# Fused GroupNorm and multi-head attention on one core: the last two batches' softmax denominators in another order, and two edits at the start

## The chip, the cores and the metric

The kernel runs on one core of a Trainium2 chip, all in float32. The metric is the device time of one execution in microseconds (us), lower is better. The kernel before takes 1836.15 us (median of three runs, 1836.12 to 1836.40). The profile shown is of one execution of it, which took 1836.99 us; the span that the profiler recorded inside it is 1835.3 us, and the granted TensorE clock was 0.997 of full speed.

The engines are named as in the profile: PE is TensorE (matrix products, with PEld its weight loads), DVE is VectorE, ACT is ScalarE, POOL is GpSimd, and SP is the sync engine, which here only issues DMA transfers. Each engine works through its own instructions in order and waits on semaphores for the others. A `q` behind an engine's name marks its queue of DMA issues and the like.

## The reference

The input x has 32 batches of 256 channels by 32x32 positions. Each batch is normalized in groups of 8 channels, projected to queries, keys and values of 8 heads of 32 channels, put through causal attention that leaves out the diagonal too, and added to x:

```python
q = einsum('oc,bcs->bos', q_w, gn(x)) + q_b        # gn: GroupNorm of 32 groups
k, v = split(einsum('oc,bcs->bos', kv_w, gn(x)) + kv_b)
scores = einsum('bhqd,bhkd->bhqk', q, k) / sqrt(32)
scores = where(mask == 0, -10000.0, scores)        # mask: tril(ones(1024, 1024), -1)
attn = where(mask == 0, 0.0, softmax(scores))
out = x + einsum('bhqk,bhkd->bhqd', attn, v)
```

## The kernel before

**Tiling.** A batch has two groups of four heads (`g`) and two halves of 512 query positions (`hf`), so its output has four quarters, numbered `n = 2 * g + hf`; each is 128 channels by 512 positions. Scores are computed transposed, keys on partitions. A batch is cut into twelve *visits*. At a visit `scores` (L290) issues the products of one full and one half piece of scores, ACT takes their exponentials (L319, L321), POOL masks what lies on the diagonal (`mask`, L283), and the products with the values (`values`, L332) of the visit before are issued. There is one running loop over `i` from 0 to 384 (32 x 12 visits and one more for the last values).

**Numerator and denominator.** TensorE adds the values' products of a quarter in one PSUM tile, and ACT copies it to `num` (L351). The softmax denominators are sums of exponentials over the keys. The keys' sum over pieces is made by DVE (`total += e`, L348), which leaves 128 partial sums for each query. There are then two ways to the end:

- *Folded*, for batches 0 to 29: `fold` (L358) adds the upper half of the partitions to the lower with an accumulating DMA from POOL, twice (512 KB, then 256 KB). `stack` (L364) brings the 32 rows that are left into one tile `folded` by a DMA from SP. `sum_folded` (L370) transposes and reduces on DVE, once for each of four heads. `check_sums` (L431) tests the range, `invert` (L437) takes the reciprocal, turns it (L446), writes it to DRAM with four small DMAs (L448) and reads it back with four broadcasts (L453, 256 KB each), which spread each head's row over its 32 partitions into `rb`.
- *Late*, for batches 30 and 31: `sums` (L401) adds up the keys with products on TensorE (`sum_keys`, L383) into the one spare PSUM bank, ACT copies it to `den` (L416), and SP writes 4 rows of it to DRAM (L419). `gather` (L424) reads them back as rows of 64, and `check_sums` and `invert` follow without the turning (one small write, L443, then the broadcasts of L453).

`finish` (L462) multiplies numerator and inverse (L466), adds the values' bias and x (L467), copies one column (L469), all on DVE, and stores the quarter (L470). In the last batch, quarters 0 and 1 go through `finish_aside` (L472) instead: POOL multiplies and adds (L477, L478), ACT adds the bias (L479), SP stores (L482). Quarters 2 and 3 of the last batch have their sums on all partitions already and are checked and inverted on the spot (`check_here` L484, `invert_here` L491, reciprocal L493). `end_last` (L495) does this for quarter 3 in two halves of 256 columns and puts one number, `outside`, together, which tells whether any sum left the range (the kernel then runs a slow general form; here it never does).

**What sets the order.** PE, ACT, DVE and POOL keep the order in which the program issues their instructions. That order is written out with `when(i, f, at)` and `when(i, f, after)`: `f` is called at visit `i`, behind its scores, or after the visit's values. The numbers stand in the tables PROJECT, PREPARE, SUMS and FINISH (L545 to L549), and the main part fills them for each batch. SP's order is set by a scheduler, mostly by when an issue's inputs are ready; the issues of SP then go out in that order too, each waiting for its own semaphores. Buffers: `folded` has one, `den` two, `rb` and the half exponentials `eh` four each.

**Start.** `load(0)` brings in x_0, `load_weights` (L122) the weights from SP and the three bias vectors from ACT's queue (L126 to L128). x_0 goes through statistics (L166), mean and variance, `norm_apply`, then the first projections, in the order of `projections` (L245), and the first scores.

Of the kernel before, what the change touches and what calls it, by code (L numbers as in the profile page):

```python
# [17 lines left out]
P = 128  # L18
# [13 lines left out]
def tile_norm_attention_residual(  # L32
# [64 lines left out]
    def unshifted():  # L97
# [24 lines left out]
        def load_weights():  # L122
            for n, w in enumerate((q_w, kv_w[0:C], kv_w[C : 2 * C])):
                live["wn", n] = epool.tile([P, 4, HALFBANK], F32, tag="eh", bufs=4, name=f"wn_{n}")[:, :NG, :C]
                nc.sync.dma_start(out=live["wn", n], in_=w.rearrange("(o p) c -> p o c", p=P))
            nc.scalar.dma_start(out=qk_bias[:, 0, :], in_=q_b.rearrange("(g p) -> p g", p=P))  # L126
            nc.scalar.dma_start(out=qk_bias[:, 1, :], in_=kv_b[0:C].rearrange("(g p) -> p g", p=P))
            nc.scalar.dma_start(out=v_bias_col, in_=kv_b[C : 2 * C].rearrange("(g p) -> p g", p=P))  # L128

        def turn_weights(n):  # L130
            wn = live["wn", n]
# [109 lines left out]
        def projections(b):  # L241

            qk = [[lambda g=g, hf=hf, n=n: project_qk(b, g, n, hf) for n in range(2)] for g in range(NG) for hf in range(NH)]
            v = [lambda n=n: project_v(b, n) for n in range(NB // 2)]
            return qk[0] + qk[1][:1] + v[:2] + qk[1][1:] + qk[2] + v[2:] + qk[3]  # L245

# [152 lines left out]
        def sums(b, g, hf):  # L401

            n = NH * g + hf
            den = small.tile([P, HALF], F32, tag="den", name=f"den_{b}_{n}")
            if (b, n) == (B - 1, 3):
                pd = live["pd", b]
            else:
                pd = misc(f"pd_{b}_{n}")
                sum_keys(pd, live.pop(("sum", b, g, hf)), slice(0, HALF), slice(0, HALF))
            if b == B - 1 and n >= 2:  # L410

                most = small.tile([P, 1], F32, tag="most", name=f"most_{n}")
                nc.scalar.activation(den, pd, AF.Identity, accum_out=most)
                live["most", n], live["den", n] = most, pd if n == 3 else den
                return
            nc.scalar.copy(den, pd)  # L416
            if n == 0:
                live["sums", b] = dram.tile([4, 4, HALF], F32, tag="sums", name=f"sums_{b}")
            nc.sync.dma_start(out=live["sums", b][n], in_=den[::HD, :])  # L419
# [17 lines left out]
        def invert(b, ns):  # L437
            part = slice(ns.start * HD, ns.stop * HD)
            inv = small.tile([P, ROW], F32, tag="inv", name=f"inv_{b}_{ns.start}")
            nc.vector.reciprocal(inv[part], live["rows", b][part])  # L440
            live["inv", b] = dram.tile([4, 4, HALF], F32, tag="inv", name=f"inverses_{b}_{ns.start}")
            if b >= B - 2:
                nc.sync.dma_start(out=spread_rows(live["inv", b])[part], in_=inv[part])  # L443
            else:
                turned = small.tile([P, ROW], F32, tag="inv_turned", name=f"inv_turned_{b}")
                nc.vector.transpose(turned, inv)  # L446
                for n in ns:
                    nc.sync.dma_start(  # L448
                        out=live["inv", b][n].rearrange("(a j) (m c) -> (j m) a c", a=2, c=HD),
                        in_=turned[n * HD : (n + 1) * HD].rearrange("p (a c) -> p a c", a=2),  # L450
                    )
            for n in ns:
                nc.sync.dma_start(  # L453
                    out=inverses(b, n),
                    in_=live["inv", b][n].unsqueeze(1).broadcast_to([4, HD, HALF]),
                )

        def inverses(b, n):
            live["rb", b, n] = work.tile([P, HALF], F32, tag="rb", bufs=4, name=f"rb_{b}_{n}")
            return live["rb", b, n]  # L460

        def finish(b, n, within=slice(0, HALF)):  # L462
# [6 lines left out]
                nc.vector.tensor_copy(rb[:, 0:1], xt[:, g, 0:1])  # L469
            nc.sync.dma_start(out=x_out[b, :, g, cols], in_=rb)  # L470

        def finish_aside(b, n, within=slice(0, HALF)):  # L472

            g, hf = divmod(n, NH)
            cols = slice(hf * HALF + within.start, hf * HALF + within.stop)
            num, rb, xt = live["num", b, n], live["rb", b, n][:, within], live["x", b]
            nc.gpsimd.tensor_tensor(rb, num[:, within], rb, ALU.mult)  # L477
            nc.gpsimd.tensor_tensor(rb, rb, xt[:, g, cols], ALU.add)  # L478
            nc.scalar.activation(rb, rb, AF.Identity, bias=v_bias_col[:, g : g + 1])  # L479
            if cols.start == 0:  # L480
                nc.scalar.copy(rb[:, 0:1], xt[:, g, 0:1])
            nc.sync.dma_start(out=x_out[b, :, g, cols], in_=rb)  # L482

        def check_here(n, ok):  # L484
# [4 lines left out]
            nc.vector.scalar_tensor_tensor(ok, live["most", n], SUM_MAX, least, ALU.is_le, ALU.mult)  # L489

        def invert_here(b, n, within):  # L491
            rb = live["rb", b, n] if within.start else inverses(b, n)
            nc.vector.reciprocal(rb[:, within], live["den", n][:, within])  # L493

        def end_last(b):  # L495

# [1 line left out]
            worst = const.tile([P, 1], F32, name="worst")  # L498
            ok = const.tile([P, 1], F32, name="ok")
            nc.vector.tensor_reduce(worst, in_range, AX.X, ALU.min)  # L500
            check_here(3, ok)
            both = [slice(c * HALFBANK, (c + 1) * HALFBANK) for c in range(2)]
            invert_here(b, 3, both[0])
            pc = ps_o.tile([P, HALF], F32, tag="acc", name="pc")
            nc.tensor.matmul(pc[0:1, 0:1], lhsT=worst, rhs=ok, start=True, stop=True)
            outside = const.tile([1, 1], I32, name="outside")
            nc.vector.tensor_scalar(outside, pc[0:1, 0:1], -1.0, float(P), ALU.mult, ALU.add)
            finish_aside(b, 3, both[0])
            invert_here(b, 3, both[1])
            finish(b, 3, both[1])  # L510
            return outside

# [30 lines left out]


        PROJECT = (-5, -4, -3, -2, -1, 0, 1, 2, 3, 4, 5, 6)  # L545
        PREPARE = (-16, -15, -9, -9, -8, -8, -7, -6, -5, -4)
        SUMS = (3, 7, 9, 13)

        FINISH = ((N + 13, N + 13, N + 14, N + 15), (N + 7, N + 7, N + 8, N + 9))  # L549
        every = range(4)  # L550

        with tc.manual_schedule(engines={ENG.PE, ENG.Activation, ENG.DVE, ENG.Pool}):
# [7 lines left out]
            keep_busy(11)  # L560
            for g in range(NG):
                norm_channels(0, g)
            nc.vector.tensor_scalar_mul(qk_bias[:, 0, :], qk_bias[:, 0, :], SCALE)
            norm_mean(0)
            keep_busy(3)
            norm_deviation(0)
# [5 lines left out]
            for hf in range(NH):  # L572
                for g in range(NG):
                    norm_apply(0, hf, g)
            units = projections(0)
            for n, f in zip((None, None, 0, 0, 0, 0) + PROJECT[6:], units):
                if n is None:
                    f()
                else:
                    when(n, f)  # L580
            if B > 1:
                prepare(1, (None, None, 0, 1, 2, 2, 3, 4, 5, 6))
            for b in range(B):
                first, last, late = b * N, b == B - 1, b >= B - 2
                if b >= 1:
                    for n, f in zip(PROJECT if not last else PROJECT[:-1] + (8,), projections(b)):
                        when(first + n, f)
# [2 lines left out]
                    prepare(b, [first + n for n in PREPARE])  # L590
                for n in every:
                    v = first + (N if last and n == 3 else SUMS[n])
                    if late:
                        when(v, lambda b=b, n=n: sums(b, *divmod(n, NH)), after)
                    else:
                        when(v, lambda b=b, n=n: fold(b, n, 2 * HD), after)
                        when(v + 2, lambda b=b, n=n: fold(b, n, HD), after)
                        when(v + 4, lambda b=b, n=n: stack(b, n))
                if not last:
                    if late:  # L600
                        when(first + N + 2, lambda b=b: gather(b, every))
                    else:
                        when(first + N + 6, lambda b=b: sum_folded(b, every[:2]), after)
                        when(first + N + 7, lambda b=b: sum_folded(b, every[2:]), after)
                    v = first + N + (4 if late else 8)
                    when(v, lambda b=b: check_sums(b, every))
                    when(v, lambda b=b: invert(b, every))
                    for n in every:
                        when(first + FINISH[late][n], lambda b=b, n=n: finish(b, n), after)
                else:  # L610
                    when(first + N - 4, lambda b=b: gather(b, every[:2]))
                    when(first + N - 3, lambda b=b: check_sums(b, every[:2]))
                    when(first + N - 3, lambda b=b: invert(b, every[:2]))
                    when(first + N, lambda b=b: check_here(2, in_range[:, ROW : ROW + 1]))
                    when(first + N, lambda b=b: invert_here(b, 2, slice(0, HALF)))
                    when(first + N, lambda b=b: finish(b, 2))
                    for n in every[:2]:
                        when(first + N, lambda b=b, n=n: finish_aside(b, n), after)
            for i in range(B * N + 1):
                if i < B * N:  # L620
                    scores(i // N, *visits[i % N])
# [1 line left out]
                    f()  # L623
                for n, pc in enumerate(products[(i - 1) % N] if i else ()):

                    summed = i < B * N - 2 or (i == B * N - 2 and n == 0)
                    values((i - 1) // N, pc, summed)
                    if i == B * N:
                        sum_piece(B - 1, pc, stop=n == 1)
                        if n == 0:  # L630
                            sum_total(B - 1)
                if i == B * N - 1:
                    for n, pc in enumerate(products[N - 2] + products[N - 3][1:]):
                        sum_piece(B - 1, pc, start=n == 0)
                for f in after.pop(i, ()):
                    f()
# [159 lines left out]
```

## Time and profile before

| | |
|---|---|
| time, median of 3 | 1836.15 us |
| span of the profiled execution | 1835.3 us |
| one regular batch (visit to the same visit of the next) | 55.98 us |
| start of the first scores | 18.28 us |
| end of the last product | 1822.4 us |
| end of DVE's last operation | 1830.86 us |
| last store issued | 1830.89 us |

The page counts the busy time of each engine and follows back the chain of work that ended last. A row of a timeline gives the start in us, the length in us, the engine, the line of the program, the operation, what it writes and reads, and in brackets the idle time before it and what ended that. With "x4" several neighbours are merged in one row. Because the tail is short against the whole, the averages of the page say little on it; the timelines of the first 20 and the last 120 us are what bears on this change.

### The profile page before, as it was taken

Reading aid. Unit: us, or ns where it says so; the run is one execution under the profiler, and the core shown is the slowest. Engines: PE = TensorE matmul, PEld = TensorE weight load, DVE = VectorE, ACT = ScalarE, POOL = GpSimd, SP = SyncE. Lnnn points to the kernel's source line nnn. Section 1 sums busy time; section 2 is a strip of 40 time slices with the busy share of each in tenths; the row PEclk is TensorE's granted clock in tenths of the full one; section 3 lists DMA queues with packets and bytes.
Section 4 is the critical chain, followed back from the end, with each engine's and each line's share of the span. In section 5 each row is a group of like instructions: output and inputs, shape, how many; then the busy total and the mean of one; then the engine's idle time right before and its main releaser. Section 6 shows DMA issues by size and latency. Waiting matters only on the chain.

```text
span 1835.3 us, 53874 instructions
## 1 busy us (share of the span) xinstructions
PE 1815.7 (99%) x23200; PEld 925.6 (50%) x23200; DVE 1650.8 (90%) x1747; ACT 1481.1 (81%) x1871; POOL 797.1 (43%) x772
## 2 busy tenths in 40 slices
PE   8999999999999999999999999999999999999997
PEld 5454555554554555555545545555545455455443
DVE  3789999999999999999999999999999999999878
ACT  5888878888788888788887888887888877888775
POOL 1444534434434445344354344454453543444414
PEclk9999999999999999999999999999999999999999
DMA  3447676666666676766667666767667666667412
GB/s 121 69 84 137 136 154 113 127 135 139 143 127 120 136 139 136 152 113 128 135 139 145 128 121 134 139 135 152 114 125 139 137 143 133 119 134 138 88 51 84
DMA packets 77518, 231.46 MB, mean 126 GB/s; under 512 B 20288, under 2 KB 21312, under 8 KB 61912
## 3 DMA queue, kind: packets, MB, share of 16 engines
q0 software_dynamic: 15360, 94.39, 37.2%
q1 hardware_dynamic: 61096, 133.54, 24.3%
q8 instruction: 184, 3.01, 0.7%
q14 instruction: 62, 0.51, 0.1%
q10 hardware_dynamic: 816, 0.00, 0.0%
HBM read 67.42 MB, written 34.64 MB: 56 GB/s over the span
## 4 chain that ended last, share of the span: by engine, by line
PE 96%; DVE 3%; ACT 1%; issue 0%; DMA 0%; SPq 0%; DVEq 0%; ACTq 0%
PE sT L269 31%; PE acc L343 26%; PE pp L156 25%; PE ppv L156 13%; DVE e L348 1%; DVE rb L493 0%; DVE rb L466 0%; ACT e L321 0%; DMA x<-in_x_dram 0%; DVE rb L467 0%; PE pv L156 0%; ACT eh L319 0%; PE pd L383 0%; PE wt L135 0%; PE pm L156 0%
## 5 line engine op out<-in xcount | busy, mean ns | idle before, releaser
L321 ACT ACTIVATE e<-sT 128x1024 f32<-128x1024 f32 x768 | 745.9, 1025 | 274.6 <-PE sT L269 202.5
L348 DVE TENSOR_TENSOR e<-e,e 128x1536 f32<-128x1536 f32 x381 | 638.8, 1677 | 20.3 <-POOL e L283 2.7
L348 DVE TENSOR_TENSOR e<-e,eh 128x1024 f32<-128x1024 f32 x381 | 523.9, 1389 | 133.6 <-PE acc L343 113.6
L283 POOL TENSOR_SCALAR_AFFINE_SELECT e<-e 128x512 f32<-128x512 f32 (+1 forms) x256 | 379.4, 1482 | 591.6 <-ACT e L321 571.6
L269 PE MATMUL sT<-q,k 32*128 32x256 f32 (+3 forms) x7168 | 607.2, 458 | 0.8 <-ACT k L223 0.8
L269 PEld LDWEIGHTS sT<-q,k 32*128 32x128 f32 x7168 | 443.0, 184 | 158.0 <-ACT eh L319 65.6
L156 PE MATMUL pp<-xn,wT 128*32 128x512 f32 x4096 | 492.3, 598 | 0.2 <-ACT den L416 0.2
L343 PE MATMUL acc<-e,v 128*32 128x512 f32 (+2 forms) x4096 | 400.7, 486 | 0.0
L319 ACT ACTIVATE eh<-sT 128x1024 f32<-128x1024 f32 x384 | 397.6, 1036 | 0.0
L362 POOL DMA_DIRECT2D e<-e x240 | 196.6, 824 | 377.7 <-DMA e<-e 301.4
L156 PE MATMUL ppv<-wT,xn 128*32 128x256 f32 x4096 | 247.3, 382 | 0.0
L343 PEld LDWEIGHTS acc<-e,v 128*32 128x32 f32 x4096 | 132.5, 110 | 223.4 <-issue 192.1
L343 PE MATMUL acc<-eh,v 128*32 128x256 f32 x3072 | 224.4, 379 | 0.0
L156 PEld LDWEIGHTS pp<-xn,wT 128*32 128x32 f32 x4096 | 107.0, 109 | 220.0 <-issue 204.6
L343 PEld LDWEIGHTS acc<-eh,v 128*32 128x32 f32 x3072 | 98.4, 110 | 165.0 <-issue 152.9
L156 PEld LDWEIGHTS ppv<-wT,xn 128*32 128x32 f32 x4096 | 120.2, 109 | 103.1 <-issue 28.8
L283 POOL TENSOR_SCALAR_AFFINE_SELECT eh<-eh 128x512 f32<-128x512 f32 x128 | 165.8, 1295 | 0.2
L209 ACT ACTIVATE xn<-x,shift,rstd 128x512 f32<-128x512 f32 x124 | 103.3, 833 | 0.0
L467 DVE SCALAR_TENSOR_TENSOR rb<-rb,v_bias_col,x 128x512 f32<-128x512 f32 x126 | 95.8, 761 | 4.5
L223 ACT ACTIVATE q<-pp,qk_bias 128x512 f32<-128x512 f32 x128 | 91.2, 712 | 2.5 <-DVE st L166 2.5
L223 ACT ACTIVATE k<-pp,qk_bias 128x512 f32<-128x512 f32 x128 | 89.8, 702 | 2.2 <-PE pm L156 1.1
L466 DVE TENSOR_TENSOR rb<-num,rb 128x512 f32<-128x512 f32 x126 | 88.1, 700 | 0.1
(69 smaller groups left out, 671.5 us busy)
## 6 DMA issues: line engine op xcount, KB each, us to landing
e<-e POOLq DMA_DIRECT2D x120, 512.0 KB, 6.3
x<-in_x_dram SPq DMA_DIRECT2D x64, 512.0 KB
out_dram<-rb SPq DMA_DIRECT2D x127, 256.0 KB
rb<-inverses SPq DMA_DIRECT2D x126, 256.0 KB
e<-e POOLq DMA_DIRECT2D x120, 256.0 KB, 4.8
folded<-e SPq DMA_DIRECT2D x120, 256.0 KB
inverses<-inv_turned SPq DMA_DIRECT2D x120, 8.0 KB
wn<-in_L_conv_kv_w_dram SPq DMA_DIRECT2D x2, 256.0 KB
```

Of the source, the lines that this page charges most:

```text
L156: nc.tensor.matmul(out[part], lhsT=lhsT[:, part], rhs=rhs, start=start, stop=stop, skip_group_check=True)
L209: nc.scalar.activation(xn, xt, AF.Identity, bias=live["shift", b][:, g : g + 1], scale=rstd)
L223: nc.scalar.activation(live[key][:, cols], pp, AF.Identity, bias=qk_bias[:, n, g : g + 1], scale=(SCALE, 1.0)[n],)
L269: return nc.tensor.matmul(pair[:, cols], lhsT=live["k", b, g][rows, kb * P : (kb + 1) * P], rhs=live["q", b, g][rows, hf * HALF + of.start ...
L283: nc.gpsimd.affine_select(out=diagonal, in_=diagonal, pattern=[[0, 4], [0, n], [1, P]], compare_op=ALU.is_gt, fill=0.0, base=0, channel_mu ...
L319: exp = nc.scalar.activation(eh.rearrange("p (n bank) q -> p bank n q", n=2), short, AF.Exp)
L321: nc.scalar.activation(e[:, 2 * a : 2 * a + 2, :], pairs[a], AF.Exp)
L343: nc.tensor.matmul(acc[HD * j : HD * (j + 1), of], lhsT=live["v", b][:, kb, h * HD : (h + 1) * HD], rhs=e[:, j, cols], start=first, stop=l ...
L348: nc.vector.tensor_add(total[:, :, of], total[:, :, of], e[:, :, cols])
L362: nc.gpsimd.dma_start(out=total[:rows], in_=total[rows : 2 * rows], accum_op=ALU.add)
L466: nc.vector.tensor_mul(rb, num[:, within], rb)
L467: nc.vector.scalar_tensor_tensor(rb, rb, v_bias_col[:, g : g + 1], xt[:, g, cols], ALU.add, ALU.add)
```

## The change

1. The three bias loads go from ACT's queue to SP's, behind the weights. The scaling of q's bias by DVE moves from ahead of the mean to behind the first half's `norm_apply`.
2. In every batch the first V unit of the projections is issued one place earlier; for batch 0 it thereby stands ahead of the first scores. The last step of PREPARE moves one visit later.
3. Batch 30 takes the folded way like batches 0 to 29. Its sums by TensorE fall away; its folds, stacks, `sum_folded`, turning and four broadcasts come in. Its four `finish` move from visits 379, 379, 380, 381 to 381, 381, 382, 382.
4. The last batch's quarters 0 and 1 are gathered, checked and inverted one at a time (0 at visits 379 and 380, 1 at 380 and 381), into one tile `rb_last` that takes `folded`'s place. `finish_aside` is split: the part on POOL for quarter 0 goes to the end of visit 382, ahead of the masks of visit 383.
5. Check and reciprocal of quarter 2 move from visit 384 to 382. From visit 382 on the exponentials' sums of the last batch are made by TensorE alone (before, one piece of that visit was still added on DVE).
6. In `end_last` the reciprocal of the first half comes ahead of the check, and the second half's ahead of `outside`.

```diff
-            nc.scalar.dma_start(out=qk_bias[:, 0, :], in_=q_b.rearrange("(g p) -> p g", p=P))
...
+            nc.sync.dma_start(out=qk_bias[:, 0, :], in_=q_b.rearrange("(g p) -> p g", p=P))
...
-            return qk[0] + qk[1][:1] + v[:2] + qk[1][1:] + qk[2] + v[2:] + qk[3]
+            return qk[0] + v[:1] + qk[1][:1] + v[1:2] + qk[1][1:] + qk[2] + v[2:] + qk[3]
...
-            if b >= B - 2:
+            if b == B - 1:
                 nc.sync.dma_start(out=spread_rows(live["inv", b])[part], in_=inv[part])
...
+            if b < B - 1:
+                live["rb", b, n] = work.tile([P, HALF], F32, tag="rb", bufs=4, name=f"rb_{b}_{n}")
+            else:
+                if n == 0:
+                    live["rb_last"] = work.tile([P, 4, HALF], F32, tag="folded", bufs=1, name="rb_last")
+                live["rb", b, n] = live["rb_last"][:, n, :]
...
+            inverses(b, 3)
+            invert_here(b, 3, both[0])
+            quotient_aside(b, 3, both[0])
             check_here(3, ok)
-            both = [slice(c * HALFBANK, (c + 1) * HALFBANK) for c in range(2)]
-            invert_here(b, 3, both[0])
+            invert_here(b, 3, both[1])
...
-            finish_aside(b, 3, both[0])
-            invert_here(b, 3, both[1])
+            out_aside(b, 3, both[0])
             finish(b, 3, both[1])
...
-        PREPARE = (-16, -15, -9, -9, -8, -8, -7, -6, -5, -4)
+        PREPARE = (-16, -15, -9, -9, -8, -8, -7, -6, -5, -3)
...
-        FINISH = ((N + 13, N + 13, N + 14, N + 15), (N + 7, N + 7, N + 8, N + 9))
+        FINISH = ((N + 13, N + 13, N + 14, N + 15), (N + 9, N + 9, N + 10, N + 10))
...
-            nc.vector.tensor_scalar_mul(qk_bias[:, 0, :], qk_bias[:, 0, :], SCALE)
             norm_mean(0)
...
-            for n, f in zip((None, None, 0, 0, 0, 0) + PROJECT[6:], units):
+            for n, f in zip((None, None, None, 0, 0, 0) + PROJECT[6:], units):
...
-                    if late:
+                    if last:
                         when(v, lambda b=b, n=n: sums(b, *divmod(n, NH)), after)
...
+                    when(first + N + 6, lambda b=b: sum_folded(b, every[:2]), after)
+                    when(first + N + 7, lambda b=b: sum_folded(b, every[2:]), after)
+                    when(first + N + 8, lambda b=b: check_sums(b, every))
+                    when(first + N + 8, lambda b=b: invert(b, every))
...
-                    when(first + N - 4, lambda b=b: gather(b, every[:2]))
-                    when(first + N - 3, lambda b=b: check_sums(b, every[:2]))
-                    when(first + N - 3, lambda b=b: invert(b, every[:2]))
-                    when(first + N, lambda b=b: check_here(2, in_range[:, ROW : ROW + 1]))
-                    when(first + N, lambda b=b: invert_here(b, 2, slice(0, HALF)))
+                    for n in every[:2]:
+                        when(first + N - 5 + n, lambda b=b, n=n: gather(b, every[n : n + 1]))
+                        when(first + N - 4 + n, lambda b=b, n=n: check_sums(b, every[n : n + 1]))
+                        when(first + N - 4 + n, lambda b=b, n=n: invert(b, every[n : n + 1]))
+                        when(first + N - 2 + 2 * n, lambda b=b, n=n: quotient_aside(b, n), after)
+                        when(first + N - 1 + n, lambda b=b, n=n: out_aside(b, n), after)
+                    when(first + N - 2, lambda b=b: check_here(2, in_range[:, ROW : ROW + 1]))
+                    when(first + N - 2, lambda b=b: inverses(b, 2))
+                    when(first + N - 2, lambda b=b: invert_here(b, 2, slice(0, HALF)))
                     when(first + N, lambda b=b: finish(b, 2))
-                    for n in every[:2]:
-                        when(first + N, lambda b=b, n=n: finish_aside(b, n), after)
...
-                    summed = i < B * N - 2 or (i == B * N - 2 and n == 0)
-                    values((i - 1) // N, pc, summed)
+                    values((i - 1) // N, pc, i < B * N - 2)
...
-                    for n, pc in enumerate(products[N - 2] + products[N - 3][1:]):
+                    for n, pc in enumerate(products[N - 2] + products[N - 3]):
```

## The prediction

> **What bounds the kernel now.** I read the page first.
>
> ```profile
> PE 1815.7 (99%) x23200; PEld 925.6 (50%) x23200; DVE 1650.8 (90%) x1747; ACT 1481.1 (81%) x1871; POOL 797.1 (43%) x772
> PE 96%; DVE 3%; ACT 1%; issue 0%; DMA 0%; SPq 0%; DVEq 0%; ACTq 0%
> ```
>
> TensorE is busy 99% of the span and is 96% of the chain: over the body only less TensorE work, or less waiting of it, saves time. But DVE ends the chain. The chain of waits from 1815 us on is DVE without a break:
>
> ```profile
> 1814.77 2.28 DVE e L348
> ...
> 1818.74 3.27 DVE rb L493
> ...
> 1822.04 1.72 DVE rb L466
> ...
> 1828.21 1.69 DVE rb L493
> ...
> 1830.38 0.48 DVE rb L467
> ```
>
> TensorE's last product ends at 1822.4. DVE's timeline has no idle beyond 0.5 us from 1783.23 to 1830.86; then the last store is issued, and the span ends at 1835.3. So what the tail costs is read on DVE from 1783 on, not on TensorE.
>
> What the early denominators of batch 30 cost now stands in TensorE's timeline:
>
> ```profile
> 1721.45 1.04 PE L383 MATMUL pd<-e,pick 128*32 128x512 f32 x8
> 1723.20 0.24 PE L156 MATMUL pm<-mv,avg 128*32 128x2 f32 x8 [0.70 <-ACT den L416]
> ```
>
> Eight more matmuls, then a wait for ACT to empty the bank. Last, the DMA queues. SP's timeline around batch 28's inverses, and the stretches after it (us; busy PE, PEld, DVE, ACT, POOL; clock, DMA share, GB/s):
>
> ```profile
> 1747.06 2.59 SPq L448 DMA_DIRECT2D inverses<-inv_turned  x4
> 1750.40 2.58 SPq L453 DMA_DIRECT2D rb<-inverses  x4
> 1755.44 0.51 SPq L419 DMA_DIRECT2D sums<-den  x1
> ```
>
> ```profile
> 1754.00:1756.00 2.00, 2.00 (x24) 1.07 (x16) 1.90 (x2) 0.70 (x2) 0.00 (x0) 1.00 0.26 99
> 1760.00:1762.00 2.00, 2.00 (x44) 1.40 (x40) 1.90 (x2) 1.17 (x2) 0.00 (x0) 1.00 0.26 98
> 1764.00:1766.00 2.00, 2.00 (x28) 1.25 (x28) 1.98 (x1) 0.95 (x2) 0.62 (x1) 1.00 0.00 0
> ```
>
> Four broadcasts of 256 KB go at 98 GB/s with a DMA share of 0.26, that is on 4 of 16 engines: 1.05 MB / 98 GB/s = 10.7 us. The landing signals in the trace agree: first issue 1750.40, landings 1755.21, 1757.89, 1760.56, 1763.22 (4.8 us, then 2.67 each). The 8 KB write of L419 issued behind them at 1755.44 landed at 1763.40, where such a write otherwise takes 1.2 to 1.7 us.
>
> **What the skill says.** "DMA: Bandwidth & Descriptors", section "Why a DMA increments its semaphore by 16 and not by 1": a DMA from SP runs on k engines, the largest number up to 16 that divides both slowest dimensions, and on the lowest-numbered k. A broadcast whose source begins with 4 heads gets k = 4; the trace agrees (0.26). The same page, "Queues, rings and completion order": each engine takes its descriptors in ring order. So a 16-engine transfer issued behind four broadcasts has a quarter of its pieces behind them. The trace agrees: the store issued at 1814.88 landed at 1820.85, just after the broadcast ahead of it (1820.33); stores otherwise take some 1.7 us. "SBUF — State Buffer", "Who interferes with whom": a DVE operation with two SBUF inputs and a GpSimd operation that reads SBUF exclude each other. The trace agrees: L466 takes 0.68 us alone, 1.71 beside L477/L478.
>
> **The change, part by part.** Working in the clock of before's trace.
>
> *Start.* TensorE's idle of 0.81 us ahead of the first scores (they wait for `k L223`) is filled by the V unit that comes from behind them: −0.8. The bias loads are 816 packets of 4 bytes on ACT's queue between 2.96 and 7.86 us, among x_0's. x_0's second half landed at 6.98; from 2 to 5 us the core moved 209, 238 and 148 GB/s, later 330 to 400. At 350 that shortfall of 455 KB is 1.3 us. So the gain is 0 to 1.3; I take 1.0, as the chain goes from x_0 through statistics and `norm_apply` to the first product. L563 (0.12 us) leaves that chain, or lies beside it. Start: −1.8.
>
> *Batch 30 folded.* Visits of batch 30 that hold the extra sums, against the same visit of a regular batch: 363 6.89 / 5.13, 367 5.95 / 4.66, 368 4.49 / 4.22, 369 6.82 / 5.08, 373 5.90 / 4.65. The differences, 1.76 + 1.29 + 0.27 + 1.74 + 1.25 = 6.31 us, leave TensorE. Added: eight accumulating DMAs on POOL (0.82 us of issue each, POOL 43% busy; every earlier batch does it in the regular 55.98 us per batch) and four stacks on SP: hidden by TensorE. Added on DVE: four pairs of transpose and reduce, 0.70 + 0.69 each, 5.55; turning 0.24; and the rest of `invert(30)` moves from 1786.89 (0.87 us) to visit 380. They fall in the stretch where DVE never rests, so they count in full.
>
> *Last batch in two parts.* DVE: one more check and reciprocal, 0.9, since 32 rows cost about what 64 do (0.21 + 0.22 + 0.54, overlapped); the key sums of visit 381's products leave it: −2.28. TensorE gets 0.86 more of L383, hidden by DVE's tail. Net on DVE with the former part: 5.55 + 0.24 + 0.9 − 2.28 = +4.4.
>
> *The new wait, which decides.* In the built SP order the four small writes, the inverses of (31, 0), the four broadcasts of batch 30, a fifth broadcast (31, 0), and only then the gather of `rows` (31, 1) follow each other. `check_sums` of (31, 1) at visit 381 waits for that gather on DVE; queued behind it are the key sums of 381, all four `finish(30)`, the last halves and the end. Step by step:
> - `sum_folded(30)` ends: 1802.00 (where L466 stood) − 0.87 + 5.55 = 1806.7.
> - check, invert, turn: 1.15 (1745.80 to 1746.95 in batch 28): 1807.9.
> - From the end of turning to the first broadcast 2.0 to 3.5 us in the trace; I take 2.9: 1810.8.
> - Four landings by +12.8, the fifth 2.67 later, the gather with it: about 1826.5. (Alone it lands 2.2 us after issue, 1806.38 to 1808.6.)
> - DVE has check (31, 0) and the sums of 380 (0.9 + 2.4) until 1811.2, then nothing: 15.3 us idle.
> - After it: check and invert 1.0; sums of 381 2.3; four finishes 6.0 (0.68 + 0.75 each, 0.15 twice); check of 2 0.9; reciprocal 3.34; finish (31, 2) 1.6; worst 0.2; reciprocal 1.75; check of 3 0.85; reciprocal 1.75; outside 0.1; last finish 0.9: 20.7. The two POOL quotients (2.55 each) now lie beside these: from 0 to 5.1 more; I take 3.6, as half of DVE's operations there have two SBUF inputs. DVE ends at 1850.8.
> - The end follows 4.4 later (1830.86 to 1835.3): 1855.2. Less 6.31 and 1.8: 1847.1.
>
> Before's span is 1835.3 and the runs have 1836.15, 0.85 more: **1848**. That is 11.8 us slower. Its own range: gather 2 us sooner to 1 later, contention 0 to 5.1, start 0.8 to 2.1: 1843.5 to 1852.5.
>
> **Rivals.** A (same, 1838): the gather isn't held, because its pieces run beside the broadcasts. It would land at 1814.5 + 2.2 = 1816.7; DVE idles 5.5, and the end comes at 1816.7 + 20.7 + 3.6 + 4.4 − 8.1 + 0.85 = 1838.1. For: 12 of its 16 engines are free. Against: the two held transfers above.
>
> B (same to slower, 1837 to 1842): POOL decides. The quotient of (31, 0) stands ahead of visit 383's masks and waits for the fifth broadcast (1826.3); + 2.55 + 1.8 for the masks gives 1830.7; then about 4 us of values and sums, 6 of the last half's DVE work, 4.4: 1845 to 1850 − 8.1 + 0.85. It decides only when DVE comes through sooner than this.
>
> C (faster, 1832.5): nothing idles on DVE. A without its 5.5 us, or 1835.3 + 4.4 − 8.1 + 0.85: DVE's extra work eats most of what TensorE gives. For: DVE's tail is dense now, so it needs broadcasts and gather to land while DVE has other work. Against: `finish(30)`, which could fill the gap, is queued behind the waiting check. It decides if the gather is issued 5 us earlier than I read.
>
> **How the numbers follow.** Forecast 0.78, A 0.08, B's milder loss 0.08, C 0.06. Two runs differ by 0.02%, but I count 0.2% (3.7 us) as what tells from no change. Slower: 0.78 plus 0.06 of B = 0.84; same: A and 0.02 of B, 0.10; faster: 0.06. Range: forecast's 1843.5 to 1852.5 holds 0.9 of 0.78; down to 1838 it takes in B and half of A: 1838 to 1853 holds about 0.82.
>
> **What would show it.** Right: a gap of some 15 us on DVE ahead of the second L434 of batch 31, ended by a DMA on `rows`; a DMA share near 0.26 for 13 us before; scores of visit 372 starting about 8 us earlier (6.3 + 1.8); first scores with no wait for `k`. Wrong: a gap under 6 us there (A), masks of visit 383 as the last releaser of the end (B), or a chain that ends on TensorE. If visit 372 isn't 7 to 9 us earlier, the folding or start term is wrong.

## The result and the profile after

The changed kernel takes 1847.98 us (median of six runs, 1846.84 to 1848.69) against 1836.30 for the kernel before (1836.12 to 1836.75): a ratio of 1.0063, 95% interval 1.0050 to 1.0076. That is 11.7 us slower, where 11.8 was forecast. The profiled execution took 1848.65 us, with a span of 1846.9.

The totals and the chain of the page, to hold against those of before:

```profile
PE 1813.4 (98%) x23176; PEld 925.4 (50%) x23176; DVE 1658.0 (90%) x1758; ACT 1481.6 (80%) x1867; POOL 799.8 (43%) x780
PE 97%; DVE 2%; DMA 1%; SPq 0%; issue 0%; ACT 0%; DVEq 0%
```

TensorE does 2.3 us less and the span is 11.6 us longer. DMA, 0% of the chain before, is now 1% of it. The chain's own view of the last 60 us says which:

```profile
1805.88 11.54 DMA rows<-sums
...
1817.44 1.31 DVE in_range L434
```

`rows<-sums` is the gather of quarter 1 of the last batch: 8 KB, 11.54 us. DVE's timeline shows the hole that it leaves:

```profile
1799.77 2.41 DVE L348 TENSOR_TENSOR e<-e,e 128x1536 f32<-128x1536 f32 x2
1817.44 1.30 DVE L434 SCALAR_TENSOR_TENSOR in_range<-rows,in_range 32x64 f32<-32x64 f32 x1 [15.26 <-DMA rows<-sums]
...
1841.81 0.48 DVE L472 SCALAR_TENSOR_TENSOR rb_last<-rb_last,v_bias_col,x 128x256 f32<-128x256 f32 x1
```

And SP's timeline shows what was issued ahead of the gather; the stretches below it (same columns as in the prediction) show how long that took:

```profile
1799.07 1.77 SPq L448 DMA_DIRECT2D inverses<-inv_turned  x4
1800.88 0.42 SPq L443 DMA_DIRECT2D inverses<-inv  x1
1801.40 2.59 SPq L453 DMA_DIRECT2D rb<-inverses  x4
1804.04 1.79 SPq L453 DMA_DIRECT2D rb_last<-inverses  x1
1805.88 2.41 SPq L429 DMA_DIRECT2D rows<-sums  x1
```

```profile
1805.00:1807.00 2.00, 2.00 (x24) 1.07 (x16) 0.00 (x0) 1.38 (x4) 0.00 (x0) 1.00 0.26 100
...
1811.00:1813.00 2.00, 2.00 (x28) 0.78 (x24) 0.00 (x0) 1.60 (x2) 0.00 (x0) 1.00 0.26 98
...
1815.00:1817.00 2.00, 0.00 (x0) 0.00 (x0) 0.00 (x0) 0.00 (x0) 0.00 (x0) 1.00 0.18 65
```

Five broadcasts, DMA share 0.26, some 100 GB/s, until shortly before 1817.4; then the gather is there. In the last row no compute engine works at all.

The trace also has landing signals, in which the pieces of a transfer report one by one that they are in. Of the gather's 16, twelve came from 1809.60 to 1810.41 and the last four at 1816.72, 1816.86, 1817.06 and 1817.42, each 0.17 or 0.18 us behind one of the four with which the fifth broadcast ended (1816.55, 1816.68, 1816.88, 1817.24). So a quarter of the gather was held, and held to the end of the broadcasts, as the prediction had it. The issue itself took 2.41 us on SP, where that of before's gather took 0.51; no run tells what held it.

### The profile page after: what moved, and what is told of

Its sections match the earlier page's. It is cut to its first block, busy times and chain, and to the rows that moved or that the text cites. A ratio compares the mean times of both kernels' runs of the same rounds, so it can differ in the third digit from the quotient of the medians.

```text
span 1846.9 us, 53853 instructions
## 1 busy us (share of the span) xinstructions
PE 1813.4 (98%) x23176; PEld 925.4 (50%) x23176; DVE 1658.0 (90%) x1758; ACT 1481.6 (80%) x1867; POOL 799.8 (43%) x780
## 3 DMA queue, kind: packets, MB, share of 16 engines
q1 hardware_dynamic: 62136, 134.53, 24.3%
## 4 chain that ended last, share of the span: by engine, by line
PE 97%; DVE 2%; DMA 1%; SPq 0%; issue 0%; ACT 0%; DVEq 0%
PE sT L269 31%; PE acc L343 26%; PE pp L156 26%; PE ppv L156 13%; DMA rows<-sums 1%; DVE rb_last L502 0%; DVE rb L472 0%; SPq L453 0%; DVE e L348 0%; DMA x<-in_x_dram 0%; DVE rb L471 0%; PE pv L156 0%; PE wt L135 0%; DVE st L166 0%; PE busy L142 0%
## 5 line engine op out<-in xcount | busy, mean ns | idle before, releaser
L283 POOL TENSOR_SCALAR_AFFINE_SELECT e<-e 128x512 f32<-128x512 f32 (+1 forms) x256 | 374.9, 1464 | 567.3 <-ACT e L321 548.8
L362 POOL DMA_DIRECT2D e<-e x248 | 203.1, 826 | 391.4 <-DMA e<-e 292.6
L472 DVE SCALAR_TENSOR_TENSOR rb<-rb,v_bias_col,x 128x512 f32<-128x512 f32 x124 | 94.4, 762 | 4.4
L376 DVE TENSOR_REDUCE rows<-turned 128x16 f32<-128x512 f32 x124 | 85.1, 686 | 4.3
```

What stands on the lines that cost most here:

```text
L283: nc.gpsimd.affine_select(out=diagonal, in_=diagonal, pattern=[[0, 4], [0, n], [1, P]], compare_op=ALU.is_gt, fill=0.0, base=0, channel_mu ...
L362: nc.gpsimd.dma_start(out=total[:rows], in_=total[rows : 2 * rows], accum_op=ALU.add)
L376: nc.vector.tensor_reduce(live["rows", b][:, j * HALF // HD : (j + 1) * HALF // HD], turned.rearrange("p (k r) -> p k r", r=HD), AX.X, ALU ...
L472: nc.vector.scalar_tensor_tensor(rb, rb, v_bias_col[:, g : g + 1], xt[:, g, cols], ALU.add, ALU.add)
```

## The experiments

The theory, called H (held): the gather's pieces wait in the same rings behind the broadcasts, DVE waits for the gather, and everything to the end is queued behind DVE's check. Its rivals: the masks of visit 383 on POOL set the end anyway (P); DVE's added work costs it (W); the engines are busy, whatever the queue (B); folding batch 30 as such loses (F); the last batch's two-part order loses (L). The twelve kernels ran in three groups of four, each group on a chip of its own with the kernel before beside it, which took 1836.9, 1836.9 and 1836.6 us there. Each ratio is against the kernel before on the same chip. Single runs spread more (1834.6 to 1838.6), so I rest on the intervals and on the traces.

**The gather first.** One line of the program, one visit earlier:

```diff
-                        when(first + N - 5 + n, lambda b=b, n=n: gather(b, every[n : n + 1]))
+                        when(first + N - 5, lambda b=b, n=n: gather(b, every[n : n + 1]), (at, after)[n])
```

> The changed kernel, with the gather of (31, 1) called at the end of visit 379, so that SP issues it between batch 30's small writes and thus ahead of its four broadcasts. Theory H (held: the gather's pieces stand behind the broadcasts in the same rings): it lands some 2 to 4 us after issue, by 1803; DVE's gap of 15.26 us ahead of the check of (31, 1) shrinks under 3 us. The small write of (31, 0) now goes behind the broadcasts, so the fifth broadcast comes 1 to 2 us later and the masks of visit 383 with it; the end is then set by them: TensorE done at about 1827.5, then 5.6 us of DVE's last half and 4.5 to the end: 1839, between 1836 and 1841. Theory P (the masks on POOL, for which TensorE waited 6.36 us, set the end anyway): 1847 to 1850. Theory W (DVE's added work, and not the wait, is what costs): not under 1845.

Measured: 1842.21 us (1839.71 to 1842.84), ratio 1.0027 (1.0018 to 1.0036); its profiled execution took 1840.95. DVE's, TensorE's and again DVE's timeline:

```profile
1800.63 0.21 DVE L434 SCALAR_TENSOR_TENSOR in_range<-rows,in_range 32x64 f32<-32x64 f32 x1
```

```profile
1822.22 1.93 PE L343 MATMUL acc<-e,v 128*32 128x384 f32 x16 [8.76 <-POOL e L283]
```

```profile
1828.89 1.76 DVE L502 RECIPROCAL rb_last<-pd 128x256 f32<-128x256 f32 x1 [7.38 <-ACT den L413]
```

The gap of 15.26 us is gone: the check follows the sums of visit 380 without a wait. With it goes somewhat over half of the loss (5.3 us are left, where the changed kernel, run again below, has 12.4), and the masks take the place: the fifth broadcast is issued only at 1812.86, because the small writes of quarters 0 and 1 now stand behind the four; it holds up the POOL quotient, the quotient the masks, and the masks TensorE. W falls, and P as the cause of the whole; P as the next wait is seen. The median is 1.2 us above the range given for it.

**The masks freed too.** In addition:

```diff
-                        when(first + N - 2 + 2 * n, lambda b=b, n=n: quotient_aside(b, n), after)
-                        when(first + N - 1 + n, lambda b=b, n=n: out_aside(b, n), after)
+                        when(first + N, lambda b=b, n=n: quotient_aside(b, n), after)
+                        when(first + N, lambda b=b, n=n: out_aside(b, n), after)
```

> As the kernel with the gather first, and in addition the POOL quotients of quarters 0 and 1 both behind visit 384, so that visit 383's masks no longer stand behind them. There the masks ended the chain: DVE was ready at 1821.5 and waited 7.4 us for the last quarter's sums. Theory H with the masks as second wait: DVE goes on at once, TensorE ends by 1817, and the time falls by 6 to 7.4 us from the 1842.2 of that run, to 1835 (1834 to 1837). If the masks only stood beside another wait of the same length, 1840 to 1843.

Measured: 1835.27 us (1833.57 to 1837.33), ratio 0.9991 (0.9982 to 1.0000). The same reciprocal, in DVE's timeline, now 5.9 us earlier and with no wait ahead of it:

```profile
1823.00 1.75 DVE L502 RECIPROCAL rb_last<-pd 128x256 f32<-128x256 f32 x1
```

So two waits on the same broadcasts, one behind the other, make the change slower than the kernel before: the gather's, then the masks'. With both out it is no slower.

**The gather on another queue.** Issued from ACT at visit 381, while SP's broadcasts run:

```diff
-            nc.sync.dma_start(out=live["rows", b][part], in_=spread_rows(live["sums", b])[part])
+            queue = nc.scalar if ns.start == 1 else nc.sync
+            queue.dma_start(out=live["rows", b][part], in_=spread_rows(live["sums", b])[part])
...
-                        when(first + N - 5 + n, lambda b=b, n=n: gather(b, every[n : n + 1]))
+                        when(first + N - 5 + 2 * n, lambda b=b, n=n: gather(b, every[n : n + 1]))
```

> The changed kernel, with the gather of (31, 1) issued from ACT's queue at visit 381, when the broadcasts are under way on SP's. Theory H, in the form that only the order within SP's own rings holds it: it lands 2 to 5 us after issue although the broadcasts run, the gap on DVE is under 5 us, and the end is set by visit 383's masks as above, 1838 (1836 to 1841). Theory B (what holds the gather is that the four engines are busy, whatever the queue): it lands with the last broadcast, the gap stays at 12 to 16 us, 1846 to 1849.

Measured: 1839.19 us (1837.02 to 1841.44), ratio 1.0011 (1.0004 to 1.0018). ACT's queue, DVE, and two stretches:

```profile
1803.63 0.36 ACTq L430 DMA_DIRECT2D rows<-sums  x1
```

```profile
1808.39 0.21 DVE L435 SCALAR_TENSOR_TENSOR in_range<-rows,in_range 32x64 f32<-32x64 f32 x1 [5.96 <-DMA rows<-sums]
```

```profile
1805.00:1807.00 2.00, 2.00 (x26) 0.98 (x18) 0.00 (x0) 1.62 (x4) 0.00 (x0) 1.00 0.28 104
...
1813.00:1815.00 2.00, 2.00 (x32) 0.74 (x24) 1.93 (x4) 1.04 (x2) 0.00 (x0) 1.00 0.26 97
```

Lines count from L430 on one more than in the changed kernel. The same transfer, issued into the same traffic, lands 4.7 us after issue and not 11.5, while the broadcasts go on at 97 GB/s for more than 5 us after it has landed. Twelve of its landing signals came by 1806.31, the last four from 1808.06 to 1808.36, before the second of the five broadcasts had ended (1809.20). B falls: it is the order within SP's queue that holds the gather. Busy engines do slow it (4.7 us here; the kernel before's gather of 16 KB, alone, took 2.2). The Trainium skill, "DMA: Bandwidth & Descriptors", section "Queues, rings and completion order", says that an engine takes turns between the queue rows that have work for it, packet by packet, and that SP and ACT each own one row. This run agrees as far as the gather got in between the broadcasts' pieces; it doesn't show single packets. Of the loss 2.3 us are left: DVE still idles 5.96 us ahead of the check.

**Broadcasts by head.** Each of four DMAs takes one head of all quarters, and `rb` is one tile of four quarters:

```diff
             for n in ns:
+                inverses(b, n)
+            for j in range(4):
                 nc.sync.dma_start(
-                    out=inverses(b, n),
-                    in_=live["inv", b][n].unsqueeze(1).broadcast_to([4, HD, HALF]),
+                    out=live["rb_all"][HD * j : HD * (j + 1), ns.start : ns.stop, :],
+                    in_=live["inv", b][ns.start : ns.stop, j, :].unsqueeze(0).broadcast_to([HD, ns.stop - ns.start, HALF]),
                 )
...
+                live["rb_all"] = work.tile([P, 4, HALF], F32, tag=tag, bufs=1, name=f"rb_{b}")
+            live["rb", b, n] = live["rb_all"][:, n, :]
```

> The changed kernel, in every batch with each group of four broadcasts cut by head and not by quarter: each reads one head's rows of all quarters and writes 32 partitions, so that both sides begin with 32 and not with 4. Order of issue as in the changed kernel. Theory H with 16 engines for each: the DMA share during the broadcasts rises from 0.26 to above 0.6, they end in 3 to 6 us in place of 13, the gather lands with them by 1808, the gap on DVE shrinks to 2 to 6 us, and the time to 1836 to 1840. If 32 partitions are written no faster than 4 engines did before, share and time stay: 1846 to 1849. Theory P or W: not under 1845 in either case.

Measured: 1836.85 us (1834.91 to 1837.29), ratio 1.0000 (0.9991 to 1.0009). A stretch of the broadcasts, SP's timeline and DVE's:

```profile
1803.00:1805.00 2.00, 2.00 (x28) 1.01 (x18) 1.85 (x2) 1.59 (x3) 0.00 (x0) 1.00 1.02 206
```

```profile
1799.60 0.36 SPq L429 DMA_DIRECT2D rows<-sums  x1
1800.15 3.61 SPq L455 DMA_DIRECT2D rb<-inverses  x8
```

```profile
1801.17 0.21 DVE L434 SCALAR_TENSOR_TENSOR in_range<-rows,in_range 32x64 f32<-32x64 f32 x1 [0.77 <-DMA rows<-sums]
...
1807.74 0.70 DVE L471 TENSOR_TENSOR rb<-num,rb 128x512 f32<-128x512 f32 x1 [2.88 <-DMA rb<-inverses]
```

The share goes from 0.26 to 1.02, so all 16 engines work, at 206 GB/s: twice the rate, not four times. The order of issue did not stay as I had written: with this edit the scheduler put the gather ahead of the broadcasts. So the run gives the rate of the other form of broadcast, but says nothing on a gather behind faster broadcasts. The time is as expected, for a reason that is half another one: the gather's wait shrinks to 0.77 us by the order. The masks' shrinks to 0.35 us on TensorE (8.76 with the gather first), by the rate or by the order, which this run doesn't part.

**Part 3 alone.** The kernel before, with batch 30 folded:

```diff
-                first, last, late = b * N, b == B - 1, b >= B - 2
+                first, last, late = b * N, b == B - 1, b == B - 2
...
-                    if late:
+                    if last:
                         when(v, lambda b=b, n=n: sums(b, *divmod(n, NH)), after)
```

with `sum_folded`, `check_sums`, `invert` and FINISH as in the changed kernel.

> The kernel before, with only part 3 of the change (batch 30 folded, its finish at visits 381 and 382). In this build SP issues the gather of (31, 0) and (31, 1), still one transfer, ahead of batch 30's broadcasts. Theory H (only a transfer behind the broadcasts is held): no gap on DVE over 4 us at the check of batch 31, and the end worked out from before's tail with DVE's added work and the later broadcasts: 1839.5 (1838 to 1842). Theory F (folding batch 30 as such costs what the change lost): 1848 to 1850, as no gain of the start is in it. If the 6.3 us of TensorE came through: 1830.

Measured: 1841.78 us (1841.04 to 1842.95), ratio 1.0030 (1.0018 to 1.0041). DVE:

```profile
1805.42 0.22 DVE L434 SCALAR_TENSOR_TENSOR in_range<-rows,in_range 64x64 f32<-64x64 f32 x1 [1.60 <-DMA rows<-sums]
...
1823.71 3.35 DVE L493 RECIPROCAL rb<-den 128x512 f32<-128x512 f32 x1 [1.92 <-DMA out_dram<-rb]
```

The gather, ahead of the broadcasts, keeps DVE for 1.60 us only. Still the fold loses 4.9 us: DVE has 5.55 us more to do, waits four times for batch 30's broadcasts (0.41, 1.01, 1.20, 0.42), and once for a store to release a buffer of `rb`. The 6.3 us that TensorE gains are used up. F is right in sign, and wrong in size: not 12 us.

**Everything but part 3.** The changed kernel with batch 30 late again; gather, check and FINISH for it as in the kernel before, all else as changed:

```diff
-                    if last:
+                    if last or late:
                         when(v, lambda b=b, n=n: sums(b, *divmod(n, NH)), after)
```

> The changed kernel without part 3: batch 30 takes the late way as before, all else as changed. Four of five broadcasts are then long done, and the gather of (31, 1) stands ahead of the fifth. Theory H: no gap of DVE there over 3 us; DVE has 1.4 us less of work than before, the start gives some 2.5: 1833 (1831.5 to 1834.5). Theory L (the last batch's two-part order loses by itself): 1837 or more.

Measured: 1830.57 us (1830.29 to 1831.55), ratio 0.9968 (0.9957 to 0.9980): 6.3 us faster than before, 2.4 faster than I expected, and below my range. DVE:

```profile
1805.64 0.21 DVE L434 SCALAR_TENSOR_TENSOR in_range<-rows,in_range 32x64 f32<-32x64 f32 x1
...
1818.88 1.75 DVE L502 RECIPROCAL rb_last<-pd 128x256 f32<-128x256 f32 x1
```

Neither waits. L falls: the last batch's new order gains, as the start alone gives only some 3 us (below). This version beats both kernels. Of the 2.4 us, 1.67 stand in the profiled execution's start: its first product comes at 10.82 us, in the changed kernel, which has the same start, at 12.49. Why, the part on the start says.

Now the parts can be added up, each against the kernel before beside it: part 3 alone +4.9, all but part 3 −6.3, sum −1.4. The changed kernel was run again, in the third group:

> The changed kernel as it is, on the chip of the experiments, so that they compare on one chip: 1848 to 1849.5 against 1836.9 for the kernel before, with the gap of some 15 us on DVE. A gap under 10 us would mean that the wait isn't the same in each execution.

Measured: 1848.94 us (1847.27 to 1851.20), ratio 1.0065 (1.0048 to 1.0081), or +12.4; the gap on DVE is 15.29 us. So some 13.7 us of the change's time belong to no part alone, but to the two together, in the one order of issue that puts the gather behind five broadcasts. The kernel with the gather first and the masks freed, where both waits are out, is at −1.6, close to the sum of the parts. Starts of kernels that share the same edits there differ by up to 2 us (next part), so such sums are good to about that.

**The start.** Parts 1 and 2 of the change, in the kernel before, together and one at a time (the lines are those of the diff in the section on the change):

> The kernel before, with only parts 1 and 2 of the change (biases on SP behind the weights, V unit ahead of the first scores, the last step of PREPARE one visit later). From the forecast 1.8 us less than before, from the starts of visits in the two traces 2.2 to 2.5 us less: 1834.0 (1833.6 to 1834.6). If the tail's own waits take the gain back, 1836.

> The kernel before, with only part 1 (the biases' loads on SP behind the weights, the scaling behind the first norm_apply). From the forecast 1.0 us for x_0, from the two traces the first product 1.35 us earlier (13.84 to 12.49): first product at 12.3 to 12.9, a visit late in the run (360, 1702.95 before) 1.0 to 1.5 earlier, time 1 to 1.5 less than before. If the weights, which now share the queue with the biases, come later and hold the first product, no gain.

> The kernel before, with only part 2 (V unit ahead of the first scores). TensorE's idle of 0.81 us ahead of the first scores goes, nothing else: the first product at 13.84 as before, visit 360 0.8 us earlier (up to 1.1 if a later wait goes with it), time 0.8 less than before, which these runs can hardly tell. If the V unit's PSUM or ACT copy holds the scores, the gain is below 0.4.

Measured: together 1833.78 us, ratio 0.9982 (0.9975 to 0.9989), so some 3 us less (2.0 to 4.6); biases alone 1834.19, ratio 0.9988 (0.9982 to 0.9995), some 2 less; V unit alone 1835.25, ratio 0.9995 (0.9988 to 1.0002), some 1 less, not told from nothing by the times. In its trace the first scores have no wait for `k` any more.

The traces didn't show what I expected. With the biases alone the first product came at 13.89 us and visit 360 only 0.2 earlier (1702.77), though x_0 was there at 4.78; that execution was one of the slowest of its 20 (1836.89). With the V unit alone the first product came at 13.24, not 13.84, and visit 360 1.85 earlier (1701.10), not 0.8. The reason lies mostly between the product of the mean and the first product of the projections, above all in the 12 transposes of the weights there. Biases alone, then everything but part 3:

```profile
9.86 2.82 PE L135 MATMUL wt<-ident,wn 128*128 128x128 f32 x12
```

```profile
8.62 1.53 PE L135 MATMUL wt<-ident,wn 128*128 128x128 f32 x12
```

They took 1.53 us in five of the 14 traces and 2.3 to 2.8 in the other nine, and from the mean's product to the first product it was 3.6 us in the five and 4.9 to 6.0 in the nine. In the five the granted clock was 1.00 from 8 to 14 us; in eight of the nine it fell to between 0.50 and 0.56 in one of those stretches of 2 us, in that of the biases alone no fall is recorded. Kernels with the same start are in both groups, so the edits there aren't what parts them; I take it for scatter between executions. The times with the gather first fall into two groups too, 1839.7 to 1841.0 and 1842.2 to 1842.8. Free of it: from the first product to the first scores of batch 1 it is 64.84 us before, and 63.96 both with the V unit alone and in the changed kernel, so the V unit gives 0.88, as forecast. And the product of the mean starts at 8.36 to 8.68 us in the three traces with the biases on ACT's queue and at 7.25 to 7.85 in the eleven with them on SP's, which is about 1 us, as forecast. What the times show beyond these two stays open.

**Two tries at a faster version.** First, the broadcasts by head, the quotients late, check and reciprocal of quarter 2 ahead of batch 30's finish, and a third buffer for `den`:

```diff
-        FINISH = ((N + 13, N + 13, N + 14, N + 15), (N + 9, N + 9, N + 10, N + 10))
+        FINISH = ((N + 13, N + 13, N + 14, N + 15), (N + 10, N + 10, N + 10, N + 10))
...
-            den = small.tile([P, HALF], F32, tag="den", name=f"den_{b}_{n}")
+            den = small.tile([P, HALF], F32, tag="den", bufs=3, name=f"den_{b}_{n}")
```

> A version that should beat both. The changed kernel with the broadcasts by head, the POOL quotients of quarters 0 and 1 behind visit 384, all of batch 30's finish behind visit 382's values, so that check and reciprocal of quarter 2 (4.2 us on DVE) fill the wait for the broadcasts, and three buffers for den, so that TensorE doesn't wait 2.79 us for ACT's copy of (31, 1). From the run with broadcasts by head: DVE's last operation at 1828.3; less 2.9 of gap, less some 1.5 of contention with POOL: 1824, that is 4.4 us under that run: 1832.4 (1830 to 1834), against 1836.9 for the kernel before. If the finish and not the gap is what ends last, no gain: 1836 to 1837.

Measured: 1833.22 us (1831.82 to 1835.81), ratio 0.9980 (0.9973 to 0.9986). It beats both kernels, but not the version without part 3. Second, that version with the quotients late:

> The fastest version so far (changed kernel, batch 30 late) with the POOL quotients of quarters 0 and 1 both behind visit 384. In it L471 and L472 took 1.58, 1.17, 1.65 and 1.68 us where they take 0.68 and 0.75 alone, about 3.2 us too much on DVE. If the POOL operations of these quotients are what shares the port, some 1.5 of it goes and the rest moves on to the last quarters: 1829.5 (1828.5 to 1831). If the quotients then end last, on ACT and the stores: 1831 to 1833.

Measured: 1830.46 us (1830.13 to 1832.44), ratio 0.9967 (0.9954 to 0.9979): no gain over 1830.57. The sharing with POOL left `finish` of quarter (30, 3) (1.17 and 0.75 us in place of 1.17 and 1.65), but DVE then waited for TensorE's last sums:

```profile
1818.92 1.76 DVE L502 RECIPROCAL rb_last<-pd 128x256 f32<-128x256 f32 x1 [0.78 <-ACT den L413]
```

What DVE saved up to there, it waited. The two engines' ends stand within 1 us of each other in this version.

## Why the prediction was right

By its own steps. The trace of after runs 8.8 us ahead of the clock that the sum was worked in (visit 374 starts at 1765.77, before at 1774.57), and I take that off below.

- *Batch 30's sums leave TensorE, 6.31 us.* Visit 360, ahead of them, starts 2.48 us earlier (1700.47 against 1702.95), visit 374, behind them, 8.80: 6.32.
- *Start, 1.8 us.* Too small: 2.48 at visit 360, and some 3 (2.0 to 4.6) by the times of the start alone, past the top of its range, 2.1. The first product comes 1.35 us earlier (12.49 against 13.84), where I had taken 1.0, but that is one pair of traces with the scatter of the start in it; over all traces the biases give about 1. The V unit's 0.8 was 0.88, and 0.25 more follows later.
- *End of sum_folded* 1806.7 − 8.8 = 1797.9; it was 1797.8. *First broadcast* 1802.0; it was 1801.40.
- *Gather* 1826.5 − 8.8 = 1817.7; DVE went on at 1817.44. *Gap* 15.3; it was 15.26.
- *The rest on DVE* 20.7 + 3.6 = 24.3 us; it was 1841.81 + 0.48 − 1817.44 = 24.85. The share of POOL is in it: L434 and L435 took 1.30 us each beside the first quotient, not 0.21, and L472 and L471 1.63 and 1.56 beside the second.
- *To the end* 4.4; it was 4.6. Span 1847.1 forecast, 1846.9 measured.

So the mechanism and its steps were right, and part of the closeness is luck. With the start's 2.48 in place of 1.8 the sum would be 0.7 lower, and the other terms were 0.5 short. The 0.85 from span to time was luck too: before's profiled execution took 1.69 us more than its span and was 0.84 above the median, and the changed kernel's happened to lie 0.67 above its own. One reading was off without bearing on the sum: stores land 2.0 to 2.2 us after issue near the end of before's trace, not some 1.7; the held one took 5.97.

Rival A (not held) would have needed the gather on another queue; as the order was, it was held. Its 1838 is near what the run with ACT's queue gave. Rival B is in the trace as the masks' wait for the fifth broadcast:

```profile
1821.11 1.93 PE L343 MATMUL acc<-e,v 128*32 128x384 f32 x16 [6.36 <-POOL e L283]
```

It didn't decide, since DVE reached the last half only at 1837, late as the forecast had it; with the gather out of the way it decided by 7.4 us. Rival C's 1832.5, 3.7 us under the kernel before, was reached only by versions that undid more than the hold: 3.6 and 6.3 under it.

One thing the forecast missed. `sum_folded` and the copies to `den` share two buffers, so in the changed kernel ACT's copy of (31, 1) waits for DVE's transpose, and TensorE for ACT:

```profile
1797.16 3.34 PE L156 MATMUL pp<-xn,wT 128*32 128x512 f32 x16 [2.79 <-ACT den L416]
```

By the trace it cost nothing here, because TensorE waited 6.36 us for the masks later; no run tested it alone. But I had put no cost on it, and hadn't looked for it.

## What to carry to other kernels

Ask of every small transfer that an engine waits for which large transfers stand ahead of it in the same queue: here broadcasts that begin with four rows kept to about 4 of 16 engines (share 0.26), and a group of five, 1.3 MB, held 8 KB until 11.5 us after its issue. Issue the small one first or on another queue, and look again at the built order after each edit, since a scheduler may turn it over. And where one engine (here DVE) ends the chain, work taken from the busiest engine (here 6.3 us of TensorE) buys nothing if it comes back as work for the one that ends it.

## What the runs showed of the hardware that I had not expected

After the 2.79 us that TensorE waited for `den`, its clock was down: stretch 1797 to 1799 of the changed kernel, and the same stretch of the version with a third `den` buffer, where the wait was 0.32 us:

```profile
1797.00:1799.00 2.00, 1.83 (x12) 0.52 (x16) 1.86 (x7) 2.00 (x4) 0.00 (x0) 0.50 0.05 12
```

```profile
1797.00:1799.00 2.00, 2.00 (x32) 1.30 (x28) 1.86 (x7) 1.79 (x4) 0.00 (x0) 1.00 0.00 0
```

The 16 matmuls behind the wait took 3.34 us in the one and 1.92 in the other, so the wait cost TensorE half as much again. So it was in all seven traces with a wait of 2.79 us there (3.02 to 3.56 us). The Trainium skill, "TensorE: Matmul & The Clock Gate", section "Part 1: The HAM clock gate (the "warmup" mystery)", describes such a gate, which halves the clock after an idle window of about 3.4 us. Here the drop came with a shorter wait. But the length of the wait alone doesn't set it: with part 3 alone, TensorE later waited 2.90 us, the clock stayed at 1.00 (stretches from 1817 to 1823), and the matmuls behind it kept their usual pace:

```profile
1821.05 1.07 PE L383 MATMUL pd<-e,pick 128*32 128x512 f32 x8 [2.90 <-DVE e L348]
```

What else decides, these runs leave open.

The broadcasts by head, each into 32 partitions, reached 206 GB/s with a share of 1.02; the loads at the start of the changed kernel moved 401 GB/s from 4 to 5 us with a share of 0.99. All engines busy was not all of the bandwidth. The Trainium skill, "SBUF — State Buffer", section "Door 1: The DMA port swizzle (why `[64,N]` ≈ `[32,N]`)", gives about 218 GB/s as the limit for a transfer into partitions 0 to 31 (189 measured for 1 MiB), as these reach 8 of 16 ports. The 206 fits that; no run here tells the ports from another limit.
